# A decoder layer with sixteen experts: seven batches sorted in one group, and every expert on every token of the last batch

## The chip, the core and the metric

The kernel runs on one core of one Trainium2 chip. The metric is device time in microseconds; the time before is the median of five runs. All data are 32-bit floats.

The engines named here are PE (matrix multiply, with PEld its weight loads), DVE and ACT (elementwise work), POOL (elementwise work and the indirect DMAs, which it issues itself) and SP, whose queue issues most of the other DMAs. ACT issues a few DMAs too.

## What is computed

Eight batches of 512 tokens, width 256, go through one layer in three parts, each on a layer norm of `x` and added to `x`: an attention whose weights are rolled copies of one softmax (a convolution over the tokens), a causal cross attention on a context, and a feed-forward part with sixteen routed experts, of which each token uses two, and two shared experts.

```python
gs = jnp.einsum('td,ndm->tnm', flat, wg_s)
us = jnp.einsum('td,ndm->tnm', flat, wu_s)
out = jnp.einsum('tnm,nmd->td', jax.nn.silu(gs) * us, wd_s)
probs = jax.nn.softmax(flat @ router_w, axis=-1)
weights, indices = jax.lax.top_k(probs, TOP_K)
weights = weights / (weights.sum(axis=-1, keepdims=True) + 1e-09)
comb = jnp.sum(jax.nn.one_hot(indices, N_ROUTED) * weights[..., None], axis=1)
g = jnp.einsum('td,edm->tem', flat, wg_r)
u = jnp.einsum('td,edm->tem', flat, wu_r)
h = jax.nn.silu(g) * u
h = h * comb[:, :, None]
out = out + jnp.einsum('tem,emd->td', h, wd_r)
```

A routed expert has 64 hidden channels, a shared one 128. `comb` is zero for fourteen of the sixteen experts of a token, so a kernel may leave those out by sorting tokens by expert, or work them all and multiply by zero.

## The kernel before

**Batches.** The loop over `b` emits one iteration per batch. The string ORDER names its steps in order: `c00` to `s1` the convolution (L398 to L417), `p0 p1` its projection and the second norm (L432, L240), `sc`, `pt`, `at` the cross attention (L450, L467, L479), `t30 t31` the transposed input of the feed-forward part (`x2T`, L256 to L261), `lg rt` the router. Names with `+` are the first steps of the next batch (its values L338, queries L354, context values L366, and `z`, which writes 40 KB to DRAM and loads the four T tiles from it, L312 and L318). Names with `-` belong to the batch before: its shared experts (`h0 h1 d0 d1`, L614 to L633) and its sort (`rk`, `sd0` to `sd7`).

**Sort.** Batches form two groups: 0 to 5 and 6 to 7. `rk` (`ranked`) counts tokens per expert and gives each token and choice a row in the group's DRAM tensor `xg`; the eight sends (L588) scatter the normed rows there by indirect DMA from POOL. When the last batch of a group is sent, `tiled` and `tabled` build a table of tiles, each 128 rows of one expert. There is room for 64 tiles in group 0 and 32 in group 1; all of them are worked, empty or not.

**Quads.** Four tiles are a quad. `fetch` loads its rows (L718, SP), `pick` copies the experts' weights by a register offset (L727 on ACT; the down weights by DMA, L737 on SP and ACT), `turn` transposes (L753), `hidden` (L772 to L776) and `down` (L786 to L799) compute, and four `put`s (L807, POOL) scatter the weighted results to rows of `yg`. Group 0 has 16 quads, group 1 has 8. Steps of quads are interleaved with steps of batches 6 and 7 by `merged`, which deals several lists out in proportion to their lengths.

**Joins.** A batch of group 0 writes `x` to DRAM after its shared experts (`kept`, L636). At the end `keep` loads it back (L842), `take` loads the two result rows of each token from `yg` (L851, 512 KB each), `join` adds them on DVE (L860) and writes the output (L861). Batches 6 and 7 keep `x` in SBUF.

**Order of what follows batch 7.** Its rank, sends and table, interleaved with the last two of group 0's quads, the shared experts of 6 and 7, and the first joins; then group 1's eight quads beside the other joins; then the joins of 6 and 7.

**Buffers.** Tiles with the same tag share a fixed number of buffers: "gu" three PSUM tiles (L614's and the quads'), "mm" three, "tr" two; in SBUF four of "T", three of "h", three of "xs", four of "x". The queue order of an engine is not simply the written order.

Of the kernel before, what the change touches and what calls it, by code (L numbers as in the profile page):

```python
# [24 lines left out]
NMT = NRT + 2  # L25
NSH = 2

GROUPS = ((0, 1, 2, 3, 4, 5), (6, 7))

XW = D + 2  # L30
FAR = float(1 << 16)
# [34 lines left out]
ORDER = """  # L66
c00 c01 s0 c10 c11 s1 +tr0 +tr1 -rk +v0 -h0 p0 p1 -sd0 -sd1 -sd2 +v1 -h1 t20 -sd3 -sd4 -sd5 -sd6 -sd7 +z sc0 sc1 t21 +q0 pt0 sc2 pt1 
at0 sc3 at1 ++l0 pt2 +q1 at2 pt3 -d0 t30 at3 ++l1 +cv0 +cv1 +bias t31 lg -d1 rt
"""


@with_exitstack
def decoder_layer(ctx: ExitStack, tc: tile.TileContext, x, ctxT, waT, wvT, woT, bo, wkT, xwv, wqT, wr, wg, wu, wd, out):
# [202 lines left out]
    def steps_front(b):  # L276
# [12 lines left out]
        def zsoft():  # L289
            if b == 0:  # L290

                pz = ps.tile([P, 512], F32, tag="mm", bufs=3, name=f"pz{b}")
                for k in range(KC):
                    nc.tensor.matmul(pz[:H, :], wa_sb[:, k, :], s["xnT"][:, k, :], start=(k == 0), stop=(k == KC - 1))
                z = pz[:H, :].rearrange("h (i t) -> h i t", t=P)
            else:

                pz = ps.tile([P, 512], F32, tag="tr", bufs=2, name=f"pz{b}")
                for i in range(NT):
                    nc.tensor.transpose(pz[:H, i * P:(i + 1) * P], s["z"][:, i, :], ident)  # L300
                z = pz[:H, :].rearrange("h (i t) -> h i t", t=P)[:, :, ::-1]
            nm = small.tile([H, 1], F32, tag="znm", name=f"znm{b}")
            nc.vector.tensor_reduce(nm, pz[:H, :], AX.X, ALU.max, negate=True)
            zp = sb.tile([H, ZW], F32, tag="pr", bufs=2, name=f"zp{b}")
            nc.gpsimd.memset(zp[:, :P], 0.0)
            zs = small.tile([H, 1], F32, tag="zs", name=f"zs{b}")
            nc.scalar.activation(zp[:, P:].rearrange("h (i t) -> h i t", t=P), z, AF.Exp, bias=nm, accum_out=zs)
            zr = small.tile([H, 1], F32, tag="zr", name=f"zr{b}")
            nc.vector.reciprocal(zr, zs)
            s["zp_ins"] = nc.vector.tensor_scalar_mul(zp[:, P:], zp[:, P:], zr).ins  # L310
            zd = dram.tile([H, ZW], F32, tag="zd", name=f"zd{b}")
            nc.sync.dma_start(out=zd, in_=zp)  # L312
            s["T"] = []
            for q in range(H // HPT):

                t = sb.tile([P, HPT, S], F32, tag="T", bufs=4, name=f"T{b}_{q}")
                src = bass.AP(zd.tensor, zd.offset + q * HPT * ZW + 1, [[1, P], [ZW, HPT], [1, S]])
                s["T_ins"] = nc.sync.dma_start(out=t, in_=src).ins  # L318
                s["T"].append(t)
            if 2 <= b < 6:  # L320
                for g in range(2):
                    put_blanks(g, b - 2, s["T_ins"])

        steps.append(zsoft)

# [52 lines left out]
    def loaded(G, last, engine, ap, most):  # L378

        with tc.issue_after(G[last]) if last in G else nullcontext():  # L380
            return nc.values_load_multi_w_load_instructions(
                ap, [engine], min_val=0, max_val=most, skip_runtime_bounds_check_because="one-hot sums of constants and counts of rows, bounded by them")[1]


    def steps_back(b):
# [89 lines left out]
        def attend(i):  # L475
            def f():
# [9 lines left out]
                measured(s["x"], i, s["st3"])  # L486
                if i % 2 == 1:
                    s["xn3", i // 2] = normed(b, s["x"], s["st3"], 3, [i - 1, i], s["row"][0])
                    nc.gpsimd.tensor_copy(s["row"][1][:, i - 1:i + 1, 2:], s["row"][0][:, i - 1:i + 1, 2:])
            return f  # L490

        def tr3(cp):
# [16 lines left out]
        def router():  # L509
# [40 lines left out]
            for r in range(2):  # L550
                tt(s["row"][r][:, :, 1], top[r], tr, ALU.mult)
            s["oh"] = one

        def ranked():

# [48 lines left out]
    def steps_shared(b):  # L604
# [20 lines left out]
        def down(cp):  # L625
            def f():
# [4 lines left out]
                        nc.tensor.matmul(pd[:, i, :], s["h", mt][:, c * P:(c + 1) * P], wd_sb[:, mt, :], start=(mt == 0), stop=(mt == NSH - 1))  # L631
                xs = s["x"][:, 2 * cp:2 * cp + 2, :]
                nc.vector.tensor_tensor(xs, pd, xs, ALU.add)  # L633
                if cp == 1 and b in GROUPS[0]:
                    s["kept"] = dram.tile([P, NT, D], F32, tag="kept", bufs=B, name=f"kept{b}")
                    nc.scalar.dma_start(out=s["kept"], in_=s["x"])  # L636
            return f

        steps += [down(cp) for cp in range(2)]
        return named("h0 h1 d0 d1", steps)  # L640


    def tiled(g):
# [64 lines left out]
    def steps_routed(g):  # L708
# [2 lines left out]

        def fetch(q):
            def f():

                xs = sb.tile([P, QT, XW], F32, tag="T" if g else "xs", bufs=4 if g else 3, name=f"xs{g}_{q}")
                r0s = loaded(G, "sp", mybir.EngineType.SP, G["row0"][:, q * QT:(q + 1) * QT], NE * (G["n"] + P))
                for i, r0 in enumerate(r0s):
                    G["sp"] = nc.sync.dma_start(out=xs[:, i, :], in_=G["xg"][bass.ds(r0, P), :]).ins  # L718
# [61 lines left out]
        def down(q):  # L780
            def f():
                h, wdn = G["h", q], G["wdn", q]
                py = [ps.tile([P, QT // 2, D], F32, tag="gu", bufs=3, name=f"py{g}_{q}_{o}") for o in range(2)]
                for j in range(QT // 2):
                    for o in range(2):
                        nc.tensor.matmul(py[o][:, j, :], h[o * MR:(o + 1) * MR, j, :], wdn[o * MR:(o + 1) * MR, j, :], start=True, stop=True)  # L786
                if g == 0:
                    y = [sb.tile([P, D], F32, tag="y", bufs=8, name=f"y{g}_{q}_{i}") for i in range(QT)]
                else:
                    y = sb.tile([P, QT, D], F32, tag="xT", bufs=4, name=f"y{g}_{q}")  # L790
                    y = [y[:, i, :] for i in range(QT)]
                for o in range(2):
                    for j in range(QT // 2):
                        i = 2 * j + o
# [23 lines left out]
            return f  # L818

        nq = n_tiles(g) // QT  # L820
        first = [lambda: tiled(g), lambda: tabled(g), *[fetch(q) for q in range(3 + g)], pick(0), turn(0)]
        quads = []
        for q in range(nq + 2):
            x = [pick(q + 1), turn(q + 1)] if q + 1 < nq else []
# [1 line left out]
            x += [hidden(q)] if q < nq else []  # L826
            x += [put(q - 2, 3)] if q > 1 else []
            x += [down(q - 1)] if 0 < q <= nq else []
            x += [fetch(q + 3 + g)] if q + 3 + g < nq else []
            x += [put(q - 1, 0), put(q - 1, 1)] if 0 < q <= nq else []  # L830
            quads.append(x)
        return first, quads
# [1 line left out]
    def steps_join(g):  # L834
# [3 lines left out]
        def keep(bi):  # L838
            def f():
                b = GROUPS[g][bi]  # L840
                x = sb.tile([P, NT, D], F32, tag=("xn1", "ctxT", "oT")[bi % 3], bufs=1, name=f"xj{b}")
                nc.sync.dma_start(out=x, in_=st[b]["kept"])  # L842
                G["xj", bi] = x
            return f

        def take(bi):
            def f():
                y = [sb.tile([P, NT, D], F32, tag=tag, name=f"yj{GROUPS[g][bi]}_{tag}") for tag in ("qT", "v2")]
                for r in range(2):
                    rows = r * G["n"] + bi * S  # L850
                    nc.sync.dma_start(out=y[r], in_=G["yg"][rows:rows + S, :].rearrange("(p c) d -> p c d", c=NT))  # L851
                G["yj", bi] = y
# [2 lines left out]
        def join(bi):  # L855
            def f():
                b = GROUPS[g][bi]
                x, y = G["xj", bi] if g == 0 else st[b]["x"], G["yj", bi]
                for r in range(2):
                    nc.vector.tensor_tensor(x, x, y[r], ALU.add)  # L860
                nc.sync.dma_start(out=out[b].rearrange("(c p) d -> p c d", p=P), in_=x)  # L861
            return f

        n = len(GROUPS[g])
        return [keep(bi) for bi in range(n) if g == 0], [take(bi) for bi in range(n)], [join(bi) for bi in range(n)]

    where = {b: (g, i) for g, bs in enumerate(GROUPS) for i, b in enumerate(bs)}
    first, quads = steps_routed(0)
    first1, quads1 = steps_routed(1)
    ln = [[ln1(b, [0, 1]), ln1(b, [2, 3])] for b in range(B)]  # L870
    fronts, backs = [steps_front(b) for b in range(B)], [steps_back(b) for b in range(B)]
    shared = [steps_shared(b) for b in range(B)]
# [7 lines left out]
    with tc.issue_after(st[0]["zp_ins"]):  # L880
        for f in ln[1]:
            f()

    def iteration(b):
        x = dict(backs[b])
        if b > 0:
            x |= {f"-{n}": f for n, f in [*shared[b - 1].items(), *backs[b - 1].items()]}
        if b + 1 < B:
            x |= {f"+{n}": f for n, f in fronts[b + 1].items()}
        if b + 2 < B:  # L890
            x |= named("++l0 ++l1", ln[b + 2])

        ends = b == GROUPS[0][-1]
        order = ORDER.split() + (["rk", *[f"sd{i}" for i in range(8)]] if ends else [])

        late = ("-h0", "-h1", "-d0", "-d1") if b == B - 1 else ()
        return [x[n] for n in order if n in x and n not in late and not (b == GROUPS[1][0] and n[:3] in ("-rk", "-sd"))]

    def flat(x):
        return [f for y in x for f in y]  # L900

    keeps, takes, joins = steps_join(0)
    n = len(keeps)
    old = [keeps[0], takes[0], keeps[1], takes[1]]
    for i in range(n):
        old.append(joins[i])
        if i + 2 < n:
            old += [keeps[i + 2], takes[i + 2]]
    for b in range(B):
        if b + 2 < B:  # L910
            load_x(b + 2)
        now = iteration(b)
        if b == 6:
            now = merged(now, first[:1] + idle(4) + first[1:-1] + idle(22) + first[-1:] + flat(quads[:6]))
        elif b == 7:
            now = merged(now, flat(quads[6:14]))
        for f in now:
            f()
        if b == 0:
            load_blank()  # L920
        if b == 1:
            load_experts()
    last, sh6, sh7 = backs[B - 1], shared[B - 2], shared[B - 1]
    send = [last[f"sd{i}"] for i in range(8)]
    gap = flat(quads[14:])
    sh = [x[n] for x in (sh6, sh7) for n in ("h0", "h1", "d0", "d1")]
    sorting = [last["rk"], *idle(3), *send, first1[0], *idle(0), *first1[1:-1], *idle(2), first1[-1]]
    for f in merged(sorting, gap + sh, [*idle(0), *old[:5]]):
        f()
    keeps, takes, joins = steps_join(1)  # L930
    for f in merged(flat(quads1), old[5:]):
        f()
    for f in [*keeps, *takes, *joins]:
        f()


# ---- launch: one core; the host only lays data out
# [51 lines left out]
```

## Time and profile before

| | us |
|---|---|
| median of five runs | 616.9 (612.43 to 617.99) |
| the profiled execution | 618.62 |
| its span | 616.9 |
| busy PE / DVE / POOL / ACT in the span | 516.9 / 372.2 / 232.6 / 190.6 |

The times that follow are from the start of the span. Landmarks of the profiled execution:

| from | what |
|---|---|
| 101.4, 147.3, 193.4, 239.6, 286.1 | L312, once per batch: a plain batch takes 46 us |
| 313.1 | batch 6's convolution begins |
| 315.2 to 325.3 | the sends of batch 5 |
| 357.3 | first put of group 0 |
| 396.5 | batch 7's convolution begins |
| 422.9 to 438.9 | the sends of batch 6, among puts |
| 499.9 to 517.0 | the sends of batch 7, among puts |
| 545.8 to 602.4 | the last eight quads' puts |
| 604 to 617 | joins of batches 6 and 7 |

The granted clock of PE, as a share of full speed, is 1.00 in plain batches and lower in several late stretches. A row of the timeline has its start, its length, engine, line, operation, output and inputs, how many, and in brackets the idle time before it and what ended it. PE's ends are modelled, so its rows can overlap a little; starts are better for prices.

### The profile page before, as it was taken

What the parts mean: (1) busy time and instruction counts of PE and PEld (TensorE: products, weight loads), DVE (VectorE), ACT (ScalarE), POOL (GpSimd) and SP (SyncE); (2) the same over time, 40 slices, a digit from 0 to 9 for tenths busy, and PEclk for the clock granted to TensorE, in tenths of its full rate; (3) what the DMA queues carried; (4) which work ended last, traced back from release to release, by engine and by line L of the source; (5) the groups of instructions that cost most, each with busy time, mean ns of one, the idle gap of its engine ahead of it and who ended that gap; (6) DMA issues with size and microseconds to landing.
All of it is one profiled execution on the core that took longest, in us unless ns stands there. A gap on an engine that the chain in (4) does not pass through costs nothing. (4 is left out here: it accounts for less than half of the span.)

```text
span 616.9 us, 10065 instructions
## 1 busy us (share of the span) xinstructions
PE 516.9 (84%) x3172; PEld 341.1 (55%) x3172; DVE 372.2 (60%) x1290; ACT 190.6 (31%) x483; POOL 232.6 (38%) x257
## 2 busy tenths in 40 slices
PE   7989989999999999999976999988389776885610
PEld 5556546756656656656624757656256444574510
DVE  4268568687787787787765655376145562653443
ACT  2224133232232232232214444353143312153210
POOL 3202306406406406406440044537525466044670
PEclk9999999999999999999996999999679896997755
DMA  8860643822912922924815595736434142776765
GB/s 282 276 238 4 201 150 98 335 84 106 330 80 107 326 84 105 326 102 101 311 52 155 141 318 168 217 117 202 129 96 122 57 165 68 217 243 208 208 246 204
DMA packets 64108, 107.67 MB, mean 175 GB/s; under 512 B 8902, under 2 KB 37580, under 8 KB 63954
## 3 DMA queue, kind: packets, MB, share of 16 engines
q1 hardware_dynamic: 51672, 83.87, 41.4%
q0 software_dynamic: 7680, 16.87, 7.6%
q10 hardware_dynamic: 4704, 6.29, 3.1%
q8 instruction: 25, 0.41, 0.3%
q14 instruction: 27, 0.22, 0.1%
HBM read 82.35 MB, written 34.38 MB: 189 GB/s over the span
## 5 line engine op out<-in xcount | busy, mean ns | idle before, releaser
L807 POOL DMA_INDIRECT yg<-y,to x96 | 99.6, 1038 | 116.0 <-ACT y L797 80.0
L240 POOL TENSOR_TENSOR rs<-ve,power 128x2 f32<-128x2 f32 x48 | 35.3, 742 | 189.2 <-DVE ve L239 188.2
L772 PE MATMUL pgu<-xsT,wgu 128*64 128x128 f32 x768 | 63.2, 300 | 29.0 <-DVE rh L776 13.9
L588 POOL DMA_INDIRECT xg<-row,place x64 | 65.3, 1020 | 28.3 <-issue 16.8
L772 PEld LDWEIGHTS pgu<-xsT,wgu 128*64 128x64 f32 x768 | 50.2, 150 | 40.5 <-issue 38.1
L398 PE MATMUL pc<-T,vh 128*32 128x256 f32 (+1 forms) x512 | 58.1, 490 | 4.2 <-DMA T<-zd 2.0
L450 PE MATMUL psc<-kT,qT 128*128 128x128 f32 (+3 forms) x128 | 41.8, 451 | 0.9 <-DVE kT L261 0.7
L479 PE MATMUL pa<-v,pT 128*128 128x256 f32 x160 | 40.9, 385 | 0.3 <-DVE pT L470 0.3
L225 DVE BATCH_NORM_STATS2 bn<-x 128x6 f32<-128x256 f32 x96 | 37.7, 414 | 4.3 <-DMA x<-in_x_dram 3.3
L786 PE MATMUL py<-wdn,rh 64*128 64x256 f32 x192 | 33.7, 436 | 6.7 <-DMA wdn<-wdn_d 5.0
L398 PEld LDWEIGHTS pc<-T,vh 128*32 128x32 f32 x512 | 19.1, 109 | 34.2 <-issue 18.7
L338 PE MATMUL pv<-wv_sb,xr 128*128 128x272 f32 (+1 forms) x128 | 34.0, 412 | 3.9 <-ACT xr L331 3.9
L479 PEld LDWEIGHTS pa<-v,pT 128*128 128x128 f32 x160 | 29.3, 192 | 11.1 <-issue 3.6
L614 PE MATMUL pu<-x2T,wu_sb 128*128 128x512 f32 x64 | 32.3, 627 | 2.5 <-issue 2.5
L799 DVE TENSOR_SCALAR y<-py,w 128x256 f32<-128x256 f32 x48 | 22.4, 479 | 18.8 <-ACT y L797 9.5
L727 ACT COPY wgu<-wgu_r 128x256 f32 x96 | 32.3, 404 | 4.3 <-DVE oT L415 1.4
L758 DVE COPY xsT<-pxt 128x512 f32<-128x512 f32 x24 | 16.5, 687 | 28.1 <-remote 14.8
L614 PE MATMUL pg<-x2T,wg_sb 128*128 128x512 f32 x64 | 32.7, 614 | 0.9 <-DVE h L618 0.9
L631 PE MATMUL pd<-wd_sb,h 128*128 128x256 f32 x128 | 32.9, 384 | 0.0
L244 DVE TENSOR_SCALAR xn<-x,mv,rs 128x256 f32<-128x256 f32 x64 | 28.0, 476 | 6.5 <-POOL rs L240 5.5
L256 PE MATMUL pt<-ident,xn 128*128 128x128 f32 x128 | 24.2, 295 | 8.8 <-ACT xnT L259 4.4
L775 DVE SCALAR_TENSOR_TENSOR rh<-rh,pgu 128x256 f32<-128x256 f32 x24 | 10.0, 417 | 34.5 <-ACT rh L774 29.6
(174 smaller groups left out, 946.4 us busy)
## 6 DMA issues: line engine op xcount, KB each, us to landing
T<-zd SPq DMA_DIRECT2D x32, 1024.0 KB
xs<-xg SPq DMA_DIRECT2D x96, 129.0 KB
x<-in_x_dram SPq DMA_DIRECT2D x8, 512.0 KB
ctxT<-in_ctxT_dram SPq DMA_DIRECT2D x8, 512.0 KB
yj_qT<-yg SPq DMA_DIRECT2D x8, 512.0 KB
yj_v<-yg SPq DMA_DIRECT2D x8, 512.0 KB
xg<-blank SPq DMA_DIRECT2D x6, 516.0 KB
kept<-x ACTq DMA_DIRECT2D x6, 512.0 KB
```

The costliest lines, as they stand in the source:

```text
L225: nc.vector.bn_stats(stats["bn"][:, c, :], src[:, c, :])
L240: st[b].setdefault(("pow", n), []).append(nc.gpsimd.tensor_tensor(stats["rs"][:, lo:hi], ve[:, lo:hi], power[:, lo:hi], ALU.pow).ins)
L338: nc.tensor.matmul(pv[:, :w], xr[:, k, i, :], wv_sb[:, k, :w], start=(k == 0), stop=(k == KC - 1))
L398: nc.tensor.matmul(s["pc"][o][32 * g:32 * g + 32, 2 * jp * P:], vh[:, jp, h, :], s["T"][h // HPT][:, h % HPT, :S - 2 * jp * P], start=(jp ...
L450: nc.tensor.matmul(pc[:, :w], s["qT"][:, k, i * P:w], s["kT"][:, k, :w], start=(k == 0), stop=(k == KC - 1))
L479: nc.tensor.matmul(pa[:, :D], s["pT", i][:, j * P:(j + 1) * P], s["v2"][:, j, :], start=(j == 0), stop=(j == i))
L588: ins = nc.gpsimd.indirect_dma_start(out=grp[g]["xg"][:, :], out_offset=bass.IndirectOffsetOnAxis(ap=s["place"][:, r, c:c + 1], axis=0), i ...
L614: nc.tensor.matmul(p, w[:, k, mt * P:(mt + 1) * P], s["x2T"][:, k, :], start=(k == 0), stop=(k == KC - 1))
L631: nc.tensor.matmul(pd[:, i, :], s["h", mt][:, c * P:(c + 1) * P], wd_sb[:, mt, :], start=(mt == 0), stop=(mt == NSH - 1))
L772: nc.tensor.matmul(p[o * MR:(o + 1) * MR, n, j, :], wgu[:, i, n, k, :], xT[:, k, i, :], start=(k == 0), stop=(k == KC - 1))
L786: nc.tensor.matmul(py[o][:, j, :], h[o * MR:(o + 1) * MR, j, :], wdn[o * MR:(o + 1) * MR, j, :], start=True, stop=True)
L807: ins = nc.gpsimd.indirect_dma_start(out=G["yg"][:, :], out_offset=bass.IndirectOffsetOnAxis(ap=G["to", q][:, i:i + 1], axis=0), in_=G["y" ...
```

## The change

Batches 0 to 6 become one group: 72 tiles, 18 quads. Batch 7 is not sorted. Its router's two one-hot matrices, times their weights and one half, are summed to a 16-column matrix (`combed`), transposed, written to DRAM, and loaded back so that each expert's row stands in 64 partitions. The hidden layer then takes 128 columns of experts' weights at a time against all 512 tokens, eight such steps, multiplies by that matrix, and adds the two shared steps; `down` accumulates all ten in PSUM and writes batch 7's output.

Batches 4 to 7 keep `x` in SBUF. Iteration 6 loses the shared experts of 5, iteration 7 takes them, and it also takes the rank and sends of 6, the table and the first fetches; the second half of its attention is merged with the first five quads. The other quads follow, then the shared experts of 6, the dense steps, and the joins of seven batches: five pairs of loads first, the last two behind the first joins. One of a join's two adds moves to POOL.

```diff
-GROUPS = ((0, 1, 2, 3, 4, 5), (6, 7))
+GROUPS = ((0, 1, 2, 3, 4, 5, 6),)
+DENSE = (7,)
+STAY = (4, 5, 6, 7)
...
+ORDER6 = """
+c00 c01 s0 c10 c11 s1 +tr0 +tr1 -rk +v0 p0 p1 -sd0 -sd1 -sd2 +v1 t20 -sd3 -sd4 -sd5 -sd6 -sd7 +z sc0 sc1 t21 +q0 pt0 sc2 pt1
+at0 sc3 at1 pt2 +q1 at2 pt3 t30 at3 +cv0 +cv1 +bias t31 lg rt
+"""
+ORDER7 = """
+-rk --h0 c00 c01 s0 -sd0 -sd1 -sd2 -sd3 c10 c11 s1 --h1 tab p0 p1 -sd4 -sd5 -sd6 -sd7 --d0 t20 tab1 sc0 sc1 f0 f1 f2 t21 --d1 pick wd pt0 sc2 pt1 at0 turn | sc3 at1 k0 k1 k2 k3 pt2 at2 pt3 t30 at3 t31 lg rt
+"""
...
+    def combed(b, one, w, wide):
...
+        nc.sync.dma_start(out=cd, in_=cbT)
+        s["hr"] = []
+        for q in range(2):
+            t = sb.tile([P, NRT // 2, S], F32, tag="T", bufs=4, name=f"comb{b}_{q}")
+            for o in range(2):
+                nc.sync.dma_start(
+                    out=t[o * MR:(o + 1) * MR],
+                    in_=bass.AP(cd.tensor, cd.offset + (q * NRT + o) * S, [[0, MR], [2 * S, NRT // 2], [1, S]]))
+            s["hr"] += [t[:, i, :] for i in range(NRT // 2)]
...
+    def steps_dense(b):
...
+        def hidden(mt):
+            def f():
+                tag = ("mm", "gu")[mt % 2]
+                pg, pu = (ps.tile([P, 512], F32, tag=tag, bufs=3, name=f"p{n}{b}_{mt}") for n in "gu")
+                for n, p in enumerate((pg, pu)):
+                    for k in range(KC):
...
+                        nc.tensor.matmul(p, w, s["x2T"][:, k, :], start=(k == 0), stop=(k == KC - 1))
+                h = sb.tile([P, S], F32, tag="h", bufs=3, name=f"h{b}_{mt}")
+                nc.scalar.activation(h, pg, AF.Tanh, scale=0.5)
+                nc.vector.scalar_tensor_tensor(h, h, 1.0, pg, ALU.add, ALU.mult)
+                if mt < NRT:
+                    nc.vector.tensor_tensor(h, h, pu, ALU.mult)
+                    nc.vector.tensor_tensor(s["hr"][mt], s["hr"][mt], h, ALU.mult)
...
+        def down(cp):
+            def f():
+                pd = ps.tile([P, 2, D], F32, tag="tr", bufs=2, name=f"pd{b}_{cp}")
...
+                        nc.tensor.matmul(pd[:, i, :], h[:, c * P:(c + 1) * P], w, start=(mt == mts[0]), stop=(mt == mts[-1]))
+                xs = s["x"][:, 2 * cp:2 * cp + 2, :]
+                nc.vector.tensor_tensor(xs, pd, xs, ALU.add)
+                nc.sync.dma_start(out=out[b, 2 * cp * P:2 * (cp + 1) * P].rearrange("(c p) d -> p c d", p=P), in_=xs)
...
-                for r in range(2):
-                    nc.vector.tensor_tensor(x, x, y[r], ALU.add)
+                nc.gpsimd.tensor_tensor(y[0], y[0], x, ALU.add)
+                nc.vector.tensor_tensor(x, y[0], y[1], ALU.add)
...
-        if b == 6:
-            now = merged(now, first[:1] + idle(4) + first[1:-1] + idle(22) + first[-1:] + flat(quads[:6]))
-        elif b == 7:
-            now = merged(now, flat(quads[6:14]))
...
-    for f in merged(sorting, gap + sh, [*idle(0), *old[:5]]):
...
-    for f in merged(flat(quads1), old[5:]):
...
+    head, attention = iteration(B - 1)
+    for f in head:
         f()
-    for f in [*keeps, *takes, *joins]:
+    n = 5
+    for f in merged(attention, flat(quads[:n])):
         f()
+    late = [shared[B - 2][n] for n in ("h0", "h1", "d0", "d1")]
+    for f in merged(flat(quads[n:]), hiddens[:0]):
+        f()
+    for f in late + hiddens[0:] + downs:
+        f()
+    for f in takes[:5]:
+        f()
+    for i, f in enumerate(joins):
+        f()
+        if i + 5 < len(takes):
+            takes[i + 5]()
```

## The prediction

> **What bounds the kernel now.** I read first the busy time by stage (columns: stretch, its length, then busy time and count of PE, weight loads, DVE, ACT and POOL, granted clock, DMA share, GB/s).
>
> ```profile
> 140.00:200.00 60.00, 59.66 (x309) 39.06 (x308) 45.09 (x163) 18.26 (x49) 25.03 (x28) 1.00 0.44 159
> 422.00:442.00 20.00, 10.38 (x92) 7.28 (x91) 6.47 (x22) 5.67 (x15) 15.62 (x17) 0.90 0.49 157
> 442.00:460.00 18.00, 13.17 (x73) 8.69 (x72) 6.69 (x20) 5.82 (x17) 5.68 (x6) 0.69 0.38 115
> 495.00:546.00 51.00, 40.24 (x224) 25.41 (x222) 24.37 (x80) 13.05 (x33) 20.20 (x19) 0.89 0.51 159
> 546.00:602.00 56.00, 28.50 (x272) 22.96 (x268) 24.25 (x46) 15.86 (x41) 35.25 (x32) 0.75 0.71 227
> 602.00:617.00 15.00, 0.00 (x0) 0.00 (x0) 4.90 (x4) 0.00 (x0) 0.41 (x1) 0.50 0.59 210
> ```
>
> A plain batch fills PE (59.66 of 60). The late stages do not: at 422 POOL is the busy one (eight sends among the puts), and from 546 PE is half idle at a clock of 0.75. There the chain of waits runs over the puts of L807, so I read the waits from 545 to 600 (total, times, longest) and the timeline of POOL and SP's queue at the end.
>
> ```profile
> POOL yg L807 <- ACT y L797: 27.1, 6, 14.3
> PE py L786 <- DMA wdn<-wdn_d: 5.0, 1, 5.0
> ...
> 556.92 5.36 SPq L737 DMA_DIRECT2D wdn<-wdn_d  x2
> ...
> 600.16 0.97 POOL L807 DMA_INDIRECT yg<-y,to  x1 [0.31 <-issue]
> 601.44 0.97 POOL L807 DMA_INDIRECT yg<-y,to  x1 [0.30 <-issue]
> 603.56 0.34 SPq L851 DMA_DIRECT2D yj_qT<-yg  x1
> ```
>
> The second sort's quads wait for their predecessors' results and for weights that stand in SP's queue behind join traffic. The last router's numbers are ready at 494.7 and group 1's first put on this chain starts at 545.75: 51 us for one sort. The last put starts at 601.44, the first load of a join at 603.56, the span ends at 617.
>
> Last, the timeline of PE for unit prices at full clock, and two rows on order:
>
> ```profile
> 308.44 1.88 PE L614 MATMUL pu<-x2T,wu_sb 128*128 128x512 f32 x4
> 380.47 2.03 PE L772 MATMUL pgu<-xsT,wgu 128*64 128x128 f32 x32
> 384.36 1.14 PE L786 MATMUL py<-wdn,rh 64*128 64x256 f32 x8
> 387.25 1.04 PE L753 MATMUL pxt<-ident,xs 128*128 128x128 f32 x8
> 394.51 1.99 PE L631 MATMUL pd<-wd_sb,h 128*128 128x256 f32 x8
> 339.15 0.34 SPq L842 DMA_DIRECT2D xj<-kept  x1
> 311.24 0.15 DVE L546 TENSOR_TENSOR r<-r,r 128x4 f32<-128x4 f32 x1
> ```
>
> At 512 columns starts follow one another by 0.43 us (the next four of L614 start at 310.15: 1.71 / 4), at 256 by 0.22. A quad costs PE 2.03 + 1.14 + 1.04 = 4.2, less 0.1 of overlap: 4.1. The last two rows show that queues do not keep the written order: L842 of group 0 is written behind batch 7 and issued at 339; L546 runs before L537 at 311.36, which stands above it. Work that is ready moves forward. This matters below, since the new text writes the dense work and its outputs ahead of the joins.
>
> **The change, part by part.** Up to 313.1 (batch 6's first L398) nothing changes but one group's blanks.
>
> Batch 6. The period is 46.2 (L312 at 147.27, 193.43, 239.61, 286.11). Shared 5 leaves it: 16 x 0.43 + 16 x 0.22 = 10.3. That gives 36; up to 40 if the gaps it covered stay open. I take 37: 350.
>
> Batch 7 to its router. PE work: a period's 46.2, less shared 10.3 and the next front (L338 4.2, L354 3.8, L366 3.7, transposes 1.7: 13.4) is 22; plus shared 5, 10.3, plus five quads, 20.5: 53. The sort of all seven batches stands in its first half: in the rows of group 0 router's end 312.2, first send 315.2, last 324.4, first fetch 327; four of the eight sends now come behind batch 7's own L240, some 20 us in. Shared 5 and the convolution cover that; without them some 20 us of this sort would lie open. Four kept batches and the routed down weights (3.1 MB) are loaded here too, where the DMA share was 0.5 to 0.6: nothing, or 10 us at 320 GB/s if a fetch stands behind them. At a plain batch's 97% this takes 55; by the rows from 396 to 495, where 59 us of such work took 99, 88. I take 66 (80%), as the jam of sends among puts at 422 goes: no put exists yet when the sends run. Router ends at 416 (404 to 441).
>
> What is removed: rank, eight sends (8 x 1.27 of POOL = 10.2), the second table, and 24 - 18 = 6 quads: 25 us of PE, 31 of POOL, and the 51 us wait for the second sort.
>
> What is added: eight routed hidden steps of 8 matmuls x 0.43 = 3.4 us, 27.5; down 64 x 0.215 = 13.8. So PE gets 41 for the 25. With the shared part (6.9 + 3.4) the dense block is 51.5, and shared 6 before it 10.3. DVE does about 0.69 + 0.69 + 0.7 (nearest row for the last: L417, 0.53 at 384 columns) = 2.1 per step, under PE's 3.4. The broadcast weights: one 32 KB write and 2.1 MB of loads on SP's queue, about 2 (L312 to L318 at 286) + 2.1/0.32 = 9 us, covered by thirteen quads; 9 on the path if a fetch stands behind them.
>
> Quads 5 to 17. Floor per quad 4 puts x (0.97 + 0.30) = 5.1; ceiling 7.1 (545.75 to 602.41 for eight). I take 6.3: the ceiling's row has the join traffic on SP, which is gone from here. 13 x 6.3 + 5 for the trailing puts: last put at 503 (475 to 538).
>
> PE until the end: 13 x 4.1 + 10.3 + 51.5 = 115 us. Dense needs only batch 7's transposed input, so it can fill the gaps of the quads. At 97% 119, at the 79% of 495 to 546 146; I take 88%: 131, PE ends at 547. Add, output: 5 (final outputs issued at 609.70, end 617, two of them). 552.
>
> The gaps matter for the clock too: behind the 7 us gap of PE at 506 the L614 rows start 0.85 apart instead of 0.43. The Trainium skill ("TensorE: Matmul & The Clock Gate", What's actually happening) says the array drops to half rate without activity and needs about 3.4 us of sustained work to come back; by it one drop costs some 2 us, but a drop in each of thirteen quads 22, which speaks against a quad phase that dense work does not fill.
>
> Joins. Before, two batches follow the last put. Now seven: 14 loads of 0.52 MB and 7 outputs, 11 MB; the stretch 604 to 612 moves 320 GB/s: 34 us, plus 2.1 from put to first load and 5 at the end: 41. 503 + 41 = 544, beside the dense block. Each costs a POOL add of about 2.36 (L373's shape) and a DVE add of 1.22, under the 4.9 of its transfers. The Trainium skill ("SBUF — State Buffer", Who interferes with whom) says a VectorE instruction with two SBUF inputs and a GpSimd one that reads SBUF shut each other out; no row here shows it; by it a join takes 3.6, still under its transfers, and DVE's dense work is held up by 7 x 2.36 = 17 at most.
>
> Sum: max(552, 544) = 552 of span, against 616.9. The profiled run was 618.6, 1.7 above its span, the median 616.9: 554 predicted. Its own range runs from 404 + 119 + 5 + 2 = 530 to 441 + 131 + 5 + 2 = 579.
>
> **The rivals.**
>
> A. Joins behind the dense block. Batch 7's outputs are written ahead of the first join loads on SP; if the queue keeps that, or if dense steps held "gu" buffers against the quads so that the last put moves to the end of PE's work, the 41 us start at 547: 588, 590 with the rest (range 404 + 119 + 43 = 566 to 441 + 131 + 43 = 615). For it: SP works in its own order and waits there (the 5.36 above). Against: L842's early issue.
>
> B. Slower: the dense block becomes a serial stage. It is 61.8 us with shared 6, on the engine that already is the fullest. If none of it enters the quad phase, quads at 7.1 end at 416 + 92 + 5 = 513, PE is gapped as from 546 and stays at 0.75: 82, 595; joins behind it: 636, 638 as a run. It decides when the first join load issues after 623 - 41 - 2 = 580. Against it: batch 7's input is ready 87 us before the last put, and matmuls of dense work alone leave no gaps.
>
> C. Gaps fill better than I take: under 530, if the attention of batch 7 runs at 97% with the quads.
>
> D. No change: A with batch 7 at its 88 (router at 438) and PE at 88 to 82% behind it: 438 + 131 to 140 + 43 is 612 to 621.
>
> **How the numbers follow.** Main 0.58, A 0.24, B 0.09, C 0.04, D 0.05. The likeliest is 554. The range drops C and what lies above A's upper middle: 528 to 605. Five runs lie within 0.9%, so 1% is about what can be told from no change. Faster by over 1%: 0.58 + 0.24 + 0.04 = 0.86; within: 0.05; slower: 0.09.
>
> **What would show it.** Batch 7's first L398 near 350; its router near 416; 72 puts, the last near 503, with L753 rows interleaved with the wide dense matmuls; no stretch of 50 us with PE under 60%; first join load 2 us behind the last put, while dense matmuls still run; PE's last matmul near 547. A first join load behind PE's last matmul means A, or B if PE's clock is under 0.8 there. I am wrong altogether if batch 7 does not shorten although the jam at 422 is gone, or if quads without join traffic are still 7 us or more apart because something I do not see holds them.

## The result, and the profile after

The changed kernel takes 617.25 us (median, 612.82 to 625.39) beside 616.07 of the kernel before, timed with it: a ratio of 1.0055, 95% interval 1.004 to 1.0069, half a per cent longer. The forecast was 554. The profiled execution has a span of 616.3.

The busy time by stage, in the columns of the prediction's first view:

```profile
358.00:429.00 71.00, 57.80 (x418) 36.73 (x417) 39.38 (x140) 24.65 (x66) 22.60 (x24) 0.92 0.47 145
...
460.00:495.00 35.00, 24.90 (x202) 17.94 (x199) 9.46 (x25) 11.42 (x31) 17.39 (x18) 0.79 0.57 175
495.00:520.00 25.00, 22.50 (x114) 14.05 (x114) 7.29 (x20) 9.08 (x24) 9.15 (x10) 0.64 0.44 137
...
546.00:570.00 24.00, 21.82 (x59) 10.92 (x57) 13.60 (x16) 3.37 (x6) 16.54 (x11) 0.98 0.66 239
570.00:602.00 32.00, 28.00 (x79) 15.24 (x78) 23.58 (x26) 3.59 (x6) 7.29 (x3) 0.95 0.45 167
```

From 460 to 520 quads run and PE has gaps at a clock of 0.64 to 0.79; from 546 to 602 PE is nearly full (0.91 and 0.88) at a clock near 1. The work that was to fill the gaps comes behind them. The timeline (start, length) of PE's wide matmuls, of the last put, the first load of a join and the outputs of batch 7:

```profile
431.99 1.98 PE L700 MATMUL pg<-x2T,wgu_r 128*128 128x512 f32 x4
433.81 1.88 PE L700 MATMUL pu<-x2T,wgu_r 128*128 128x512 f32 x4
441.98 1.91 PE L700 MATMUL pg<-x2T,wgu_r 128*128 128x512 f32 x2
462.64 1.12 PE L700 MATMUL pg<-x2T,wgu_r 128*128 128x512 f32 x2
...
544.86 3.09 PE L653 MATMUL pg<-x2T,wg_sb 128*128 128x512 f32 x4
...
551.56 0.98 POOL L888 DMA_INDIRECT yg<-y,to  x1 [0.30 <-issue]
...
553.68 0.82 SPq L939 DMA_DIRECT2D yj<-yg  x2
...
557.25 1.88 PE L700 MATMUL pg<-x2T,wgu_r 128*128 128x512 f32 x4
...
603.81 9.01 SPq L723 DMA_DIRECT2D out_dram<-x  x2
```

Of the dense block (L700) three accumulators are computed by 464, and no more until the last quad's matmuls and the hidden layer of shared 6 (L653) are through, at 553.8. The last put starts at 551.6 instead of 503, the first join load 2 us behind it, as forecast; PE ends at 611.7 instead of 547. Of the waits from 440 to 545 (total, times, longest) this one says what the quads wait for:

```profile
ACT rh L859 <- remote: 36.5, 7, 6.1
```

Seven of the quads' tanhs (L859) wait some 5 us each for something that the view puts down to no engine of the core ("remote"). The timeline around one of them:

```profile
465.94 1.97 PE L857 MATMUL pgu<-xsT,wgu 128*64 128x128 f32 x32 [2.17 <-DVE rh L861]
466.02 0.98 POOL L888 DMA_INDIRECT yg<-y,to  x1 [2.73 <-ACT y L878]
...
469.88 0.98 POOL L888 DMA_INDIRECT yg<-y,to  x1 [0.30 <-issue]
...
471.82 0.38 ACT L859 ACTIVATE rh<-pgu 128x256 f32<-128x256 f32 x1 [4.81 <-remote]
```

PE's 32 matmuls start at 465.94 and take 1.97 us. They belong to quad 9 (counted from 0). The four puts are those of quad 7; they end at 470.86, and the tanh that needs the matmuls starts 0.96 later. From quad 7 on, nine tanhs in a row start 0.96 to 1.21 us behind the end of such puts. Two theories for the missing gain follow: **W**, the buffers that were handed out in written order kept the dense block out of the quads; **P**, puts issued back to back hold PE's results, so puts and a later quad's chain stand in series. The rival to P is **C**: the quad's own chain, with PE's half clock or the transfers, sets the pace.

### The profile page after: what moved, and what is told of

The parts are those of the page before. It is cut to its first block, busy times and chain, and to the rows that moved or that the text cites. A ratio compares the mean times of both kernels' runs of the same rounds, so it can differ in the third digit from the quotient of the medians.

```text
span 616.3 us, 9355 instructions
## 1 busy us (share of the span) xinstructions
PE 544.9 (88%) x3008; PEld 350.8 (57%) x3008; DVE 367.4 (60%) x1225; ACT 177.3 (29%) x444; POOL 211.6 (34%) x230
## 4 chain that ended last, share of the span: by engine, by line
PE 60%; DVE 11%; issue 8%; DMA 6%; another core or an unknown queue 4%; ACT 4%; POOL 3%; SPq 1%; ACTq 1%; DVEq 0%; POOLq 0%
PE pc L434 8%; PE pgu L857 5%; PE psc L486 5%; PE pv L378 4%; PE pa L515 4%; PE pt L269 3%; PE po L468 3%; PE pq L366 3%; PE py L871 3%; PE pv L350 3%; DMA T<-zd 3%; PE pd L720 3%; PE pd L670 3%; PE pg L653 3%
## 5 line engine op out<-in xcount | busy, mean ns | idle before, releaser
L888 POOL DMA_INDIRECT yg<-y,to x72 | 70.8, 983 | 88.2 <-ACT y L878 69.5
L857 PE MATMUL pgu<-xsT,wgu 128*64 128x128 f32 x576 | 49.9, 325 | 19.3 <-DVE y L880 7.4
L627 POOL DMA_INDIRECT xg<-row,place x56 | 55.4, 989 | 25.1 <-issue 15.0
L857 PEld LDWEIGHTS pgu<-xsT,wgu 128*64 128x64 f32 x576 | 41.0, 165 | 28.3 <-ACT xsT L841 15.2
L468 PE MATMUL po<-wo_sb,oT 128*128 128x256 f32 x128 | 29.8, 382 | 0.7 <-DVE late L450 0.7
L366 PE MATMUL pq<-ctxT,qk_sb 128*128 128x512 f32 x64 | 30.3, 593 | 0.0
L838 PE MATMUL pxt<-ident,xs 128*128 128x128 f32 x144 | 27.8, 318 | 2.6 <-DMA xs<-xg 2.6
L378 PE MATMUL pv<-xwv_sb,ctxT 128*128 128x256 f32 x128 | 28.9, 379 | 0.0
L653 PE MATMUL pg<-x2T,wg_sb 128*128 128x512 f32 x56 | 28.8, 618 | 0.0
L670 PE MATMUL pd<-wd_sb,h 128*128 128x256 f32 x112 | 28.8, 381 | 0.0
L350 PEld LDWEIGHTS pv<-wv_sb,xr 128*128 128x128 f32 x128 | 23.7, 190 | 8.5 <-ACT xr L343 4.5
```

What stands on the lines that cost most here:

```text
L350: nc.tensor.matmul(pv[:, :w], xr[:, k, i, :], wv_sb[:, k, :w], start=(k == 0), stop=(k == KC - 1))
L366: nc.tensor.matmul(pq, qk_sb[:, k, m * P:(m + 1) * P], s["ctxT"][:, k, :], start=(k == 0), stop=(k == KC - 1))
L378: nc.tensor.matmul(pv[:, i, :], s["ctxT"][:, k, j * P:(j + 1) * P], xwv_sb[:, k, :], start=(k == 0), stop=(k == KC - 1))
L468: nc.tensor.matmul(po[:, i, :], s["oT"][:, k, c * P:(c + 1) * P], wo_sb[:, k, :], start=(k == 0), stop=(k == KC - 1))
L627: ins = nc.gpsimd.indirect_dma_start(out=grp[g]["xg"][:, :], out_offset=bass.IndirectOffsetOnAxis(ap=s["place"][:, r, c:c + 1], axis=0), i ...
L653: nc.tensor.matmul(p, w[:, k, mt * P:(mt + 1) * P], s["x2T"][:, k, :], start=(k == 0), stop=(k == KC - 1))
```

## The experiments

The runs were made in sets, each with the kernel before timed beside it, and the sets were of two kinds: in some the kernel before took 575 us, in others, as where the result was measured, 616 to 621 (575 sets and 616 sets below). The expectations put this down to the chip. The record doesn't show that: it gives the 575 sets the chip numbers 1, 3, 13 and 14, and the later 616 sets 13 and 15, so that number 13 stands for both kinds. What makes the difference stays open. The changed kernel was run again in sets of both kinds. "Apart" is the distance of the tanhs of quads 5 to 17, the span of these starts by twelve; PE's end is that of the last L720 row.

| run | before there | ratio (95%) | apart | last put | PE's end | span |
|---|---|---|---|---|---|---|
| the changed kernel, result | 616.1 | 1.0055 (1.004 to 1.007) | 8.69 | 551.6 | 611.7 | 616.3 |
| after_third, the same | 618.5 | 1.006 (1.000 to 1.012) | 8.71 | 551.9 | 612.4 | 617.1 |
| after_again, the same | 575.7 | 1.003 (1.000 to 1.006) | 5.94 | 508.2 | 566.9 | 571.5 |
| one_put_filled | 575.7 | 0.981 (0.970 to 0.993) | 6.01 | 500.0 | 560.5 | 564.5 |
| one_put_fourth | 618.5 | one time, 576.2 | 5.91 | 509.7 | 570.4 | 574.4 |
| shared6_early | 574.9 | 1.015 (1.008 to 1.022) | 6.02 | 523.5 | 572.4 | 577.1 |
| fill | 574.9 | 0.998 (0.994 to 1.001) | 8.06 | 532.7 | 546.0 | 573.3 |
| fill_more | 620.9 | 0.971 (0.963 to 0.980) | 9.06 | 561.3 | 575.0 | 601.0 |
| own_buffers | 575.2 | 1.003 (1.000 to 1.007) | 6.25 | 512.5 | 568.5 | 573.2 |
| sends_first | 575.7 | 0.996 (0.992 to 1.000) | 6.27 | 507.1 | 566.2 | 570.9 |
| joins_dve | 575.2 | 0.993 (0.990 to 0.996) | 6.09 | 511.0 | 565.2 | 569.8 |
| sends_part | 575.7 | 0.965 (0.957 to 0.974) | 6.53 | 506.5 | 549.1 | 553.3 |
| part_dve | 574.6 | 0.9525 (0.949 to 0.956) | 6.65 | 509.4 | 545.6 | 549.8 |
| part_dve_more | 620.9 | 0.9535 (0.945 to 0.962) | 8.58 | 551.7 | 585.9 | 590.2 |

**The changed kernel in sets of both kinds.** No edit.

> The changed kernel itself, unchanged, so that the other runs of this set have it on their own chip: the kernel before took 616 us where the result was measured and 575 us beside the last two kernels. Theory P (POOL's puts hold PE's results, but only on some chips): where before takes 616, this takes 616 to 620 with quads 8 us or more apart in the late stage; where before takes 575, quads are 5.5 to 6.3 apart, the last put starts near 520, and the end is 583 to 590 (shared 6 and the dense block, 67 us, behind the last quad), 1.01 to 1.03 of before. Rival (only the clock differs): the distances between puts are the same as in the result.

Up to batch 7 the two kinds agree within 3 us (first put 400.4 and 397.8); then the quads are 8.69 and 5.94 apart. In the 575 set the tanhs stand in the midst of puts:

```profile
470.31 1.97 PE L857 MATMUL pgu<-xsT,wgu 128*64 128x128 f32 x32
470.36 0.98 POOL L888 DMA_INDIRECT yg<-y,to  x1 [0.30 <-ACT xsT L841]
471.64 0.98 POOL L888 DMA_INDIRECT yg<-y,to  x1 [0.30 <-issue]
...
472.47 0.38 ACT L859 ACTIVATE rh<-pgu 128x256 f32<-128x256 f32 x1 [1.70 <-PE pgu L857]
472.93 0.98 POOL L888 DMA_INDIRECT yg<-y,to  x1 [0.30 <-issue]
```

From the start of PE's 32 matmuls to the tanh it is 2.16 us here and 5.88 above, beside the same puts. The ratio to the kernel before is the same; that kernel has such quads too where it takes 616 (its rows stand further down), and there is no profile of it from a 575 set. In the 575 set the last put comes at 508, near the forecast's 503, and PE's serial tail, 59 us from the last put to its end, takes the gain. P's distances came as expected there; its last put (520) and ratio (1.01 to 1.03) were too late and too high.

**Fewer puts.** From quad 5 on only one of a quad's four puts is left, so most routed results are missing from the output. Once in a set of each kind (and twice more in 575 sets: 564.8 and 564.1 us, quads 5.76 and 5.82 apart). Beside this edit a constant is written early to all rows of `yg`.

```diff
-            x += [put(q - 2, 2)] if q > 1 else []
+            x += [put(q - 2, 2)] if 1 < q < 7 else []
...
-            x += [put(q - 2, 3)] if q > 1 else []
+            x += [put(q - 2, 3)] if 1 < q < 7 else []
...
-            x += [put(q - 1, 0), put(q - 1, 1)] if 0 < q <= nq else []
+            x += [put(q - 1, 0), *([put(q - 1, 1)] if q < 6 else [])] if 0 < q <= nq else []
```

> Leaves out three of the four puts of each quad from quad 5 on (most rows of the routed results keep a constant that is written early, so the joined sums of seven batches lack them). Theory P: where quads of the changed kernel are 8 us or more apart, their distance falls by about 3 x 1.27 = 3.8 to 4.5 to 5.5, the tanh's waits of some 5 us per quad go, the last put comes 40 to 50 us earlier and the end falls by about as much; where they are 6 us apart, it falls only to the 4.1 to 5 that PE and its chain take, and the last put comes 10 to 20 us earlier. Theory C (a quad's own chain from PE over ACT and DVE and back sets its pace, puts or not): the distance falls by under 1 us on either kind of chip.

> As one_put_third. Where the kernel before takes 616: theory P expects quads 5 to 6.5 apart and an end at 575 to 595; the rival (transfers or clock) 8 or more. Where it takes 575: 5.7 to 6.1 apart, and the question stays open.

The 575 set keeps its distance, 6.01 for 5.94: there C is right and POOL's puts cost the quads nothing; the 2% lie behind the last tanh (496.7 for 494.1), where the last put comes 8 us sooner. In the 616 set it falls from 8.71 to 5.91, that of the other kind, and the time from 621 to 576: P. The waits that the view calls "remote" (36.8 us in seven of after_third's tanhs from 440 to 545) are gone; ACT's tanhs from 440 to 511 now wait like this, 2.6 us at most:

```profile
ACT rh L865 <- PE pgu L863: 15.9, 12, 2.6
```

The windows over quads 6 to 17, first of after_third, then of one_put_fourth:

```profile
442.00:545.00 103.00, 80.31 (x587) 55.99 (x585) 30.45 (x79) 34.35 (x90) 45.70 (x47) 0.80 0.51 146
```

```profile
442.00:511.00 69.00, 65.70 (x588) 45.23 (x587) 31.67 (x80) 35.83 (x90) 12.89 (x14) 0.98 0.61 163
```

The same matmuls (587 and 588 are recorded) take 34 us less, at a clock of 0.98 instead of 0.80. PE is 14.6 us less busy, which fits the clock (65.70 x 0.98 / 0.80 = 80.5); the other 19 were gaps.

> The changed kernel on the same chip: quads 8.7 apart and tanhs about 1 us behind the end of four puts where the kernel before takes 616; 5.9 apart, with tanhs in the midst of puts, where it takes 575, and a time within 1% of the kernel before in both cases.

It came as expected, so the pair stands in one set. What of a put does the holding, its issue on POOL or its 128 KB on the way, and what is held, the matmuls' ends or the word of them, no run tells apart.

**Shared 6 ahead of the quads.**

```diff
-    for f in merged(flat(quads[n:]), hiddens[:0]):
-        f()
-    for f in late + hiddens[0:] + downs:
-        f()
+    for f in late + flat(quads[n:]) + hiddens + downs:
+        f()
```

> Batch 6's shared part is written ahead of quads 5 to 17 instead of behind them; nothing else. Theory W (buffers of one kind are handed out in written order, so the dense block, written behind the quads, can only have the three accumulator buffers that no quad uses until the last quad has its own): shared 6 runs near 430 to 445, the dense block still stands behind the last quad but for its three buffers, and the end falls by at most shared 6's 10 us: 605 to 612, or nothing if quads slip by what shared 6 takes (617). Rival S (it is shared 6 alone, standing behind the quads, that keeps the hidden-layer buffers from the dense block): with it gone the dense block fills the quads' gaps and the end falls by 30 us or more, to 580 to 590.

The set was a 575 set, so the forecast's times can't be compared as they stand. The dense block gets five halves of accumulators in among the quads, from 445.8 to 488.4, and runs as one from 512.4: S falls. Quad 5's tanh moves from 422.9 to 436.9, and by the ratios the kernel is 1.2% slower than the changed one, a loss that W did not have.

**Shared 6 and the dense steps among the quads.**

```diff
-    for f in merged(flat(quads[n:]), hiddens[:0]):
-        f()
-    for f in late + hiddens[0:] + downs:
-        f()
+    for f in merged(flat(quads[n:]), late + hiddens):
+        f()
+    for f in downs:
+        f()
```

> Batch 6's shared part and the ten dense steps are written among quads 5 to 17, evenly spread, instead of behind them; the dense down product stays last. Theory W (as for shared6_early) expects dense rows among the quads, so PE has little left behind the last quad: 13.8 of down and an output, and the joins (37 to 41 us behind the last put) set the end. With quads 8.5 us apart as now (POOL's puts set their pace) the last put stays near 552 and the end is 590 to 597. If instead dense steps hold the accumulators that quads need, quads go to 10 or more apart, the last put goes to 570 to 580 and the end to 610 to 622: nothing won. Theory C (half clock sets the quads' chain) expects more: PE warm from the fill, quads 7 apart, last put near 535 and the end near 577.

> fill took 0.998 of the kernel before where that takes 575, with quads 8.1 apart and the joins alone behind the last put. The same again there. Where it takes 616: quads between 8.7 (the puts' pace hides the dense steps) and 10.5 (they add up), last put 552 to 575, end 593 to 616.

Dense steps now stand one to a quad, and the joins end the kernel: 40.6 us from the last put to the end of the span in the one, 39.7 in the other. In the 575 set the quads go from 5.94 to 8.06 apart, so next to nothing is won. In the 616 set they go from 8.71 to 9.06 only, as expected: there the dense steps run while quads are held, and 3% is won. The windows, first of fill, then of fill_more:

```profile
466.00:522.00 56.00, 54.02 (x419) 34.61 (x420) 31.82 (x68) 23.73 (x59) 31.11 (x30) 1.00 0.47 142
```

```profile
466.00:551.00 85.00, 75.29 (x545) 47.48 (x545) 41.65 (x91) 33.14 (x83) 39.66 (x40) 0.96 0.45 139
```

With PE at 54 of 56 us a quad plus a dense step is PE's own work in the first, 8.1 us. The second line settles the clock's part of C: at 0.96 the tanhs of quads 7 to 17 still start 0.85 to 1.5 us behind the puts.

**Own buffers for the dense block.** Nothing moves in the text.

```diff
-                tag = ("mm", "gu")[mt % 2]
-                pg, pu = (ps.tile([P, 512], F32, tag=tag, bufs=3, name=f"p{n}{b}_{mt}") for n in "gu")
+                pg, pu = (ps.tile([P, 512], F32, tag="mm", bufs=3, name=f"p{n}{b}_{mt}") for n in "gu")
...
-                h = sb.tile([P, S], F32, tag="h", bufs=3, name=f"h{b}_{mt}")
+                h = sb.tile([P, S], F32, tag="pr", bufs=2, name=f"h{b}_{mt}")
```

> The dense block's accumulators all from the three buffers that no quad uses, and its hidden rows from two buffers of the attention that is over; where it is written is unchanged (behind the quads and shared 6). Theory W (only the buffers handed out in written order kept it out of the quads): it runs in the quads' gaps, all ten steps, PE has shared 6 and 13.8 us of down left behind the last quad, and the joins set the end: 0.96 to 0.975 of the changed kernel, if quads keep their distance (5.9 us where the kernel before takes 575). Theory W2 (the buffers are half of it: where the written order is kept for what is ready at the same time, quads go first and their matmuls fill PE's queue, so only a few dense steps come in early): three or four steps move, 10 to 14 us of PE's tail, and the end falls to 0.975 to 0.985.

Six and a half accumulators instead of three run among the quads: buffers were part of what kept the block out (W2's half), but the time does not move. Behind the last put PE waits for DVE instead (two windows, then the longest of PE's waits from 515 to 545):

```profile
520.00:530.00 10.00, 5.61 (x6) 2.01 (x7) 8.84 (x7) 0.00 (x0) 9.13 (x5) 0.65 0.98 376
530.00:540.00 10.00, 7.76 (x15) 3.05 (x14) 9.47 (x9) 1.19 (x2) 7.21 (x3) 0.83 1.04 397
PE pu L699 <- DVE h L702: 7.7, 3, 5.3
```

DVE has 8.8 and 9.5 of 10 us there while PE has 5.6 and 7.8. W2's steps came, its price, 10 to 14 us, did not.

**Joins without POOL.**

```diff
-                nc.gpsimd.tensor_tensor(y[0], y[0], x, ALU.add)
+                nc.vector.tensor_tensor(y[0], y[0], x, ALU.add)
```

> The changed kernel with both adds of a join on VectorE, none on POOL. In the changed kernel the product of dense hidden rows and router weights (both operands in SBUF) takes 0.69 us alone and 2.83 beside a POOL add, and ACT's next tanh waits 12 us for DVE. If POOL's adds shut it out: no such product over 0.8 us; DVE gets seven adds of 1.22 more (8.5 us) and loses about as much in waiting, so the dense tail is 2 to 8 us shorter and the end 0.985 to 1.00 of the changed kernel. If it is the joins' transfers that slow both: still products of 2 us and more.

The product of two SBUF operands (L706; min, median, max in ns), first in after_again, then here:

```profile
L706 DVE TENSOR_TENSOR comb<-comb,h x8: 683/692/2836, 506.2 to 547.9; 128x512 f32<-128x512 f32 x8
```

```profile
L706 DVE TENSOR_TENSOR comb<-comb,h x8: 683/688/697, 517.5 to 544.0; 128x512 f32<-128x512 f32 x8
```

The 2.84 us are gone with the POOL adds, on the same transfers, and by the ratios the kernel is 1% quicker than the changed one although DVE has seven adds more.

**Sends of batch 6 in one piece** (sends_first, the first change below), and **with four of ten dense steps in the quads** (sends_part, both changes).

```diff
--rk --h0 c00 c01 s0 -sd0 -sd1 -sd2 -sd3 c10 c11 s1 --h1 tab p0 p1 -sd4 -sd5 -sd6 -sd7 --d0 t20 tab1 sc0 sc1 f0 f1 f2 t21 --d1 pick wd pt0 sc2 pt1 at0 turn | sc3 at1 k0 k1 k2 k3 pt2 at2 pt3 t30 at3 t31 lg rt
+-rk --h0 c00 c01 s0 -sd0 -sd1 -sd2 -sd3 -sd4 -sd5 -sd6 -sd7 tab c10 c11 s1 --h1 p0 p1 --d0 t20 tab1 sc0 sc1 f0 f1 f2 t21 --d1 pick wd pt0 sc2 pt1 at0 turn | sc3 at1 k0 k1 k2 k3 pt2 at2 pt3 t30 at3 t31 lg rt
...
-    for f in merged(flat(quads[n:]), hiddens[:0]):
+    for f in merged(flat(quads[n:]), late + hiddens[:4]):
         f()
-    for f in late + hiddens[0:] + downs:
+    for f in hiddens[4:] + downs:
         f()
```

> All eight sends of batch 6 stand together ahead of batch 7's second half of the convolution, and the table with them; in the changed kernel four of them start 12.5 us after the first four (377.5 behind 365.0) and the first fetch follows at 383.9. If the quads from 400 to the last put are paced by POOL and their own chain, the whole phase moves 8 to 12 us earlier, and the end with it: 0.980 to 0.988 of the changed kernel. If batch 7's attention sets it instead (its router's numbers, which the last quads do not need, or the dense block behind them), the first put comes earlier and the last one does not: 0.995 to 1.00.

> Sends as in sends_first; shared 6 and four of the ten dense steps are written among quads 5 to 17, the other six and the down product behind them. That leaves PE 6 x 3.4 + 13.8 = 34 us behind the last quad, about the 37 to 41 that the joins need behind the last put, so that neither stands alone. Theory W (written order of the buffers kept the dense block out): 10 us from the sends, and PE's tail shorter by some 27 us, less up to 10 by which the fill slows the quads: 0.95 to 0.965 of the changed kernel. If the fill slows the quads by as much as it saves behind them: 0.98 to 0.99.

The sends alone bring the first put from 397.8 to 392.0 but the last one only from 508.2 to 507.1: 0.7%, nearer the second forecast than the first. Sends and a partial fill together take 0.965: the last put stays at 506.5, and PE's end moves from 567 to 549. (sends_part_more, in one more 575 set, gave 0.9705, 0.965 to 0.976.)

**All of it.** sends_part with joins_dve's edit, in sets of both kinds.

> sends_part with both adds of a join on VectorE, as in joins_dve (which took 0.993 of the kernel before against the changed kernel's 1.003). In sends_part PE is busy 7.65 and 5.99 of 10 us in the two stretches of 520 to 540, beside the joins' POOL adds, and its last matmul ends at 552. If those gaps are DVE held by POOL's adds, they close by some 4 us and the end by 2 to 5: 0.955 to 0.965 of the kernel before. If the joins' transfers (14 loads and 8 outputs of half a MB from the last put on, 41 us) are the end by then, nothing: 0.965 to 0.972.

> part_dve took 0.9525 of the kernel before (0.949 to 0.956) where that takes 575. The same again there. Where it takes 616: if PE's dense work goes on while POOL's puts hold the quads' results, the quads stay about 8.7 apart at most, the last put is near 545 (7 us earlier by the sends), the joins follow with 41: 586 to 592, 0.95 to 0.96. If held results of dense steps slow the quads further (10 us apart), the last put is near 560 and the end 600 to 610: 0.975 to 0.99.

This beats both kernels: 547.9 us beside 574.6, 591.0 beside 620.9. In the 616 set the last put and the first join load come as in the changed kernel, but PE's tail is 26 us shorter, so that the last output of batch 7 issues at 586.7 (SP's queue, start and length):

```profile
554.02 5.21 SPq L939 DMA_DIRECT2D yj<-yg  x10
...
586.67 0.37 SPq L723 DMA_DIRECT2D out_dram<-x  x1
```

The expected 545 for the last put was wrong: the earlier sends moved nothing there (551.7), so that the time fell into its forecast by PE's tail and not by the sends.

## Why the prediction was wrong, step by step

**Batch 6** (37 us to the next convolution, 350): its convolution begins at 306.5 and the next at 358.0, 51 us, beyond the 40 allowed. The forecast took shared 5 out of this stretch. The text does, but the queue does not: all 16 matmuls of its hidden layer (L653), written in iteration 7, run here from 314.4 to 329.8. First all of PE, then L653 alone:

```profile
306.50:358.00 51.50, 44.86 (x258) 28.89 (x255) 34.01 (x137) 14.45 (x38) 14.32 (x15) 0.98 0.40 134
306.50:358.00 51.50, 7.53 (x16) 2.81 (x16) 0.98 0.40 134
```

So PE has 44.9 us of work here, not 36, and of the 6.6 idle 4.75 are one wait for batch 6's rank (L601 for DVE) ahead of the convolution. "Work that is ready moves forward" held here, against the forecast.

**Batch 7 to its router** (66 us, 53 of work at 80%): 71, with PE at 57.8 of 71, 81%. The share held, the work did not: 57.8 for 53, at a clock of 0.92, although shared 5's hidden layer had gone ahead. The later start, 8 us, and these 5 put the router at 428.8 for 416.

**Quads at 6.3, last put 503.** This is the first of the two steps that cost the gain: 8.69 where the result was measured, last put at 551.6, 49 us late, of which 13 came with the router. The floor took puts as beside the quad's chain; there they are in front of it. The ceiling of 7.1 was a mean over the eight quads of group 1, and its slowness was put down to join traffic. The row was in the profile before: where its quads follow evenly, they stand 8.4 and 7.9 apart (tanhs at 558.59, 567.00 and 574.88), and these tanhs start 0.9 to 1.4 us behind four puts:

```profile
561.03 0.97 POOL L807 DMA_INDIRECT yg<-y,to  x1 [3.86 <-ACT y L797]
...
564.86 0.97 POOL L807 DMA_INDIRECT yg<-y,to  x1 [0.31 <-issue]
...
567.00 0.38 ACT L774 ACTIVATE rh<-pgu 128x256 f32<-128x256 f32 x1 [5.41 <-PE pxt L753]
```

In the 575 set 5.94 and 508.2 are near the forecast, but by luck and not by its reason: fewer puts leave the distance as it is there.

**"Dense needs only batch 7's transposed input, so it can fill the gaps" and "work that is ready moves forward".** This is the second. From the router to PE's end it took 183 us where the forecast had 131, with PE at 0.78 up to the last put, and 60 us of it, for a forecast of 44, came behind that put. Readiness of data was not enough: a step needs its buffers, and by theory W those of "gu" and "h" stood behind all quads' and shared 6's. Own buffers let in six and a half accumulators of twenty instead of three; only a written place among the quads let in the whole block. What else holds it back when it is written last was not settled.

**PE until 547 and joins until 544, side by side.** The sum took the larger of two chains as if each ran alone. fill has the dense block where the forecast wanted it, and PE's end in a 575 set is 546; but the quads slow to 8.06, the last put goes to 532.7, and the 40 us of joins follow it. Had the dense block filled the quads where the result was measured, the time would have been near fill_more's 602, still 48 above the forecast; with the puts' hold gone but the dense block behind, near one_put_fourth's 576. So neither step alone explains the miss.

**Joins, 41 us from the last put, beside dense work**: 39.7 and 40.6 where they end the kernel. Right.

**The rivals.** What came is the first half of B, the dense block as a serial stage, without its second: the first join load at 553.7, under its point of 580. A did not come. D has the time but not the mechanism.

**The clock.** The granted clock fell to 0.80 over quads 6 to 17, and PE was 14.6 us busier than at 0.98. The Trainium skill ("TensorE: Matmul & The Clock Gate", What's actually happening) gave an estimate of 22 in the prediction; the measured figure is smaller and, as fill_more shows, not the quads' pace.

**POOL's adds.** A product of two SBUF operands took up to 2.84 us on DVE beside POOL adds, and 0.70 at most without them (joins_dve). That agrees with the rule that the prediction took from the Trainium skill ("SBUF — State Buffer", Who interferes with whom), by which it allowed an estimate of up to 17 us of delay. ACT's tanhs waited 12.2 us in all for these products in the changed kernel, and 1% of the time came back.

## What to carry to other kernels

Before filling one phase's gaps with other work, ask three things of the profile: which buffers that work takes and who is handed them first, whether the gaps survive the filling (a quad of 5.9 us with a 3.4 us dense step became 8.1), and what waits at the end of the filled phase. Price a repeated stage by its steady distance, not by a mean over its ramp and tail, and look for the instruction behind whose end each wait ends: a wait that ends a fixed time behind another engine's last instruction points at a cause where the view names none, and a run without that instruction tells.

## What the chip showed that was not expected

In the 616 sets, four puts issued back to back by POOL (4.84 us) keep ACT from seeing PE's results until about 1 us after the last (0.96 to 1.52 for quads 7 to 15 of the changed kernel's two profiles); with one of them in place of four the quads are 5.91 us apart instead of 8.71. In the 575 sets the same rows show no such thing. Nor does every indirect DMA of POOL hold every result in a 616 set: beside four sends of the result's profile (360.08 to 364.94) ACT takes results of the convolution at 362.93 and 364.43, and only the third, at 365.98, comes 1.04 behind them. Of the kernels timed in sets of both kinds, two have the same ratio to the kernel before (1.003 and 1.006; 0.9525 and 0.9535), and fill has not (0.998 and 0.971).
